# One adjacency load, one-operation masks, blockwise-turned exponentials and a re-planned order in a four-layer graph network

## The chip, the cores and the metric

The kernel runs on one core of one Trainium2 chip. The metric is the time of one execution on the device in microseconds (us). The core has five engines with a queue each: TensorE (PE, matmul), VectorE (DVE), ScalarE (ACT), GpSimd (POOL) and SyncE (SP), which here issues nearly all DMA transfers. Each engine works through its queue in order.

## The reference

128 graphs of 64 nodes with 256 features, `x` [128, 64, 256], and an integer adjacency `adj` [128, 64, 64] with entries 0 or 1. Four layers follow each other; each takes `h = relu(layernorm(x))` and adds its result to `x`:

```
layer 0  Wh = h W (4 heads of 64); e = leaky_relu(e_src[i] + e_dst[j], 0.2)
         e = where(adj > 0, e, -1e9); x += elu(softmax(e) Wh)
layer 1  the same with one head of 256 and -9e15
layer 2  relational convolution over relations 1 to 40; with entries of 0 and 1 only
         relation 1 is present: relu(adjT @ ((hW + b) * sigmoid(hWg + bg)))
layer 3  three rounds: aggr = AT (h weight_i); h = GRU(aggr, h)
out = x + h
```

All is float32. The kernel checks the adjacency's largest entry at the end and would redo everything on a general path (`general`, L1643) if it were above 1; with these inputs it is not entered.

## The kernel before

**Tiling.** Two graphs lie in one tile of 128 partitions, four such tiles make a group (`G = 4`, eight graphs), and 16 groups make the batch. Every group passes layers 0, 1 and 2 and then the three steps of the recurrence (layer 3). The steps of two neighbouring groups are interleaved: `(g, 0), (g-1, 2), (g, 1)` and so on, while the first three layers of later groups run in the gaps. The last group's steps come at the end.

**The order of the work is planned when the kernel is built.** The program's operations are recorded by `Plan.note` (the class `Plan`), each with a cost from `cost` (L583). `forward` (L328) places them engine by engine, choosing among ready operations the one with the earliest due time; `backward` (L427) derives new due times from the placement; `emit` (L503) repeats this `PASSES` times with a random generator started at `SEED` (L281), keeps the shortest plan, shifts the ranks of jobs by the listed `MOVES` (seeds for `move`, L474), places once more and issues the result. A transfer occupies SP for `ISSUE` = 665 ns in the plan and then one common wire for its bytes divided by a rate (L591). As the operations are issued from `emit`, the profile gives L549 for most of them; the products that use quarters of the array side by side are issued from `beside` (L841).

**Filler.** Where the plan foresees idle time of PE in its first 115 us, `emit` issues matmuls on a constant tile `warm` (L530, the matmul itself is L1638), whose results nobody reads: one for each 220 ns of the idle time less 100 ns.

**Loads.** `load_group` (L1298) loads a group's rows `xg` and its adjacency `at`, with the graphs of a tile pair arranged as `(t r a)`, in four transfers of 32 KB; three buffers. `load_edges` (L1312) loads the adjacency a second time as `ag`, in the order of `xg` (one transfer of 128 KB, four buffers), and a third time, transposed, as `eg`. `at` goes into the masks of layers 0 and 1, `ag` into `abd`, the recurrence's matrix (`before_recurrence`, L968).

**Masks.** `edge_bounds` (L1365) makes from `at` a matrix `m` that is `BIG` at an edge and 0 elsewhere (or `TINY` in a row without any edge). Layers 0 and 1 take the minimum of the exponentials and of `m` transposed (`mt`). It takes five VectorE operations: the row maximum `top`, its maximum `amax` for a final check of the adjacency's range, the test `top`, the product `m`, and the maximum of both.

**Exponentials.** `attention` (L1383) takes the scores `es` of the sources and targets of a group (`values`, L867, product with `w0e` or `w1e`). `exp(max(a, 0.2 a))` with `a = src + dst` is built from factors `fs`, `fd`, `gd`. For the first two groups the source factor is spread over partitions by a matmul. For the other 14 groups it is turned: ACT makes `fs` [128, n heads], PE transposes it (`tp<-ident,fs`), VectorE copies it as `fT` out of PSUM, one transfer stores `row` in DRAM, and two read it back, each for 64 partitions, as `t`. Then VectorE multiplies by `gd`, takes the maximum with `fd` and the minimum with `mt` (`t<-t,gd`, `t<-t,fd`, `t<-t,mt`), and PE multiplies with the values (`mm<-wh,t` and `mn<-wh,t`, `aggregate_graphs`, L909).

**Start.** Before the recurrence can start, group 0 passes its three layers in two halves (the second half's tiles end in `e`), and the weights of the recurrence are transposed and multiplied (`hhn`, `ihn`, `wrn`, `gn`; products `mm<-ihT,gT`). The recurrence's products go to PSUM banks `sy` and `sz`. The layer norm of the first two groups is turned by PE (`tp<-ident,hn`), that of later ones by VectorE and DMA (`way`, `hn`).

Of the kernel before, what the change touches and what calls it, by code (L numbers as in the profile page):

```python
# [10 lines left out]
F32 = mybir.dt.float32  # L11
I32 = mybir.dt.int32
# [15 lines left out]
NEG1 = -9000000000000000.0  # L28
ALPHA = 0.2
EPS = 1e-5  # L30
BIG, TINY = 3.0e38, 1.0e-24
BOUND = 6.25
NREL = 39
RC = 5
# [188 lines left out]
class Plan:  # L223
# [30 lines left out]
    def note(self, engine, call, cost, writes, reads, after=(), port=0.0, dma=False):  # L254
# [23 lines left out]
            b.ops.append(op)  # L278
        return op

    PASSES, SEED, SPREAD = 27, 39, 50.0  # L281
    MOVES = (
        10, 12, 18, 24, 27, 28, 58, 71, 83, 84, 89, 99, 118, 129, 136, 141, 144, 198, 214, 221, 266, 299, 322, 324,
        334, 341, 346, 390, 400, 412, 424, 434, 550, 559, 579, 611, 616, 682, 785, 808, 825, 869, 910, 1123, 1323,
        1710, 1729, 1754, 1784, 1908, 1924, 1933, 2133, 2158, 2174, 2755, 2883, 3921, 3988, 4026, 4270, 4596, 4876,
        4885, 5049, 5501, 5547, 5750, 5954, 6055, 6156, 6434, 6590, 7283, 7340, 7414, 7540, 7602, 7657, 7774, 7857,
        7930, 7942, 8201, 8457, 8683, 8685, 9083, 9436, 9811, 9967, 10320, 10820, 10999, 11484, 11701, 12627, 12696,
        12718, 12783, 12858, 12980, 13024, 13178, 13347, 13474, 14022, 14057, 14422, 14846, 16253, 16751, 16786,
        17194, 18227, 19571, 21611, 22526, 22951, 22990, 23107, 24055, 25299,
    )  # L290
    LEEWAY = {"PE": 100.0, "DVE": 100.0, "Activation": 100.0, "Pool": 100.0, "SP": 300.0, "-": 0.0}
    OVERLAP = {"DVE": 83.0, "Activation": 95.0, "Pool": 43.0}
# [210 lines left out]
    def emit(self):  # L503

        self.on = False
        self.link()
        best, self.random = None, Random(self.SEED)
        for _ in range(self.PASSES):
            ranks = [op.due for op in self.ops]
            end, order = self.forward()  # L510
            if best is None or end < best[0]:
                best = end, ranks, [op.start for op in self.ops]
            self.backward(end)
        end, ranks, starts = best
        jobs = list({id(op.job): op.job for op in self.ops}.values())
        for j in jobs:
            j.sum, j.count, j.shift = 0.0, 0, dict.fromkeys(self.RANKED, 0.0)
        for op, start in zip(self.ops, starts):
            op.job.sum, op.job.count = op.job.sum + start, op.job.count + 1
        for m in self.MOVES:  # L520
            self.move(m, end, jobs)
        for op, due in zip(self.ops, ranks):
            op.due = due + op.job.shift.get(op.engine, 0.0)
        end, order = self.forward()
        best = end, [(op, op.start, op.idle, op.places) for op in order]
        self.ends = best[0]
        for op, start, idle, places in best[1]:
            op.start = start
            if op.engine == "PE" and self.spare and start < 115.0 * 1e3:
                for _ in range(int((idle - 100.0) / 220.0)):  # L530
                    self.spare()
            for b, tag in places:
                b.pool.make(b, tag)
            op.call()
        self.ops = []
        return best[0]
# [46 lines left out]
def cost(engine, method, args, kwargs):  # L583

    n = elements(args[0])
    if engine == "tensor":
        m = elements(args[2] if method == "matmul" else args[0])
        return (m / 1.2 + 2.5) * (1 if method == "transpose" else 2)
    if engine == "sync" or method == "dma_start":
        to, of = args[:2]  # L590
        rate = {"way": 450.0, "fine": 220.0}.get(to.base.tag, 150.0) if isinstance(to, View) else 150.0  # L591
        if isinstance(of, View) and of.base.tag in ("way", "fine"):
            rate = 170.0 if of.base.tag == "way" else 125.0
        return n * to.shape[0] * 4 / rate
    if engine == "vector":
        if method == "bn_stats":
            return 400.0
        if method == "tensor_reduce":
            n = elements(args[1])
        plain = method == "tensor_scalar" and not any(isinstance(a, View) for a in args[2:4])  # L600
        return 150.0 + n * (0.53 if plain and n >= 512 else 1.04)
    if engine == "scalar":
        return 150.0 + 0.86 * n if method in ("copy", "mul") else 310.0 + 0.73 * n
    if ALU.pow in args:
        return 1000.0
    return 200.0 + 2.1 * n if method != "memset" else 100.0 + 0.85 * n
# [3 lines left out]
def kernel(  # L610
# [33 lines left out]
    xr = x.rearrange("b n d -> (b n) d").rearrange("(t q) d -> q t d", q=P)  # L644
    ar = adj.rearrange("b n m -> (b n) m").rearrange("(t q) m -> q t m", q=P)

    tr = adj.rearrange("(t r a) i j -> t a i r j", r=2, a=2)
    er = adj.rearrange("(t r a) j i -> t r j a i", r=2, a=2)
    outr = out.rearrange("b n d -> (b n) d").rearrange("(t q) d -> q t d", q=P)

# [7 lines left out]

    same = nc.kept(const, [P, P], F32, name="same")
    diag = nc.kept(const, [P, N], F32, name="diag")  # L660
    amax = nc.kept(const, [P, NG], F32, name="amax")
    flag = nc.kept(const, [1, 1], I32, name="flag")
    wc = nc.kept(const, [P, LAYERS, K, 3 * D], F32, name="wc")
    whh = nc.kept(const, [P, K, 3 * D], F32, name="whh")
# [554 lines left out]
    with ExitStack() as s1:  # L1219
# [47 lines left out]
        class Layer:  # L1267
# [2 lines left out]

            place = {"em": "hn", "dg": "hn", "tb": "hn", "land": "hn"}

            shared = {"hn": 3, "o": 2, "st": 4, "mv": 4, "var": 4, "rstd": 4, "nm": 4, "rec": 4, "fT": 1}

            def __init__(self, layer, pool, bufs):
                self.layer, self.pool, self.bufs = layer, pool, bufs
# [16 lines left out]
        for i, a in enumerate((a_src, a_dst)):  # L1293
            nc.scalar.dma_start(AB[:, i, :], over_partitions(a, D))
        nc.scalar.dma_start(w0e[:, :, :D], rows(W0))
        AT, XG, AG, EG = [], [], [], []

        def load_group(g):  # L1298
            nc.begin(("load", g))
            xg = work.tile([P, G, D], F32, name="xg", bufs=5)  # L1300
            n = 2 if g == 0 else G
            for p in range(0, G, n):
                nc.sync.dma_start(xg[:, p : p + n], xr[:, g * G + p : g * G + p + n, :])
            at = work.tile([P, G // 2, 2, N], I32, name="at", bufs=3)
            for a in range(2):
                for u in range(G // 2):
                    edges = tr[g * G // 2 + u, a]
                    nc.sync.dma_start(at[a * N : (a + 1) * N, u], edges)
            AT.append(at)
            XG.append(xg)  # L1310

        def load_edges(g):  # L1312
            ag = work.tile([P, G, N], I32, name="ag", bufs=4)
            nc.sync.dma_start(ag, ar[:, g * G : (g + 1) * G, :])
            AG.append(ag)
            eg = work.tile([P, G, N], I32, name="eg", bufs=2)
            for r in range(2):
                for u in range(G // 2):
                    nc.sync.dma_start(eg[r * N : (r + 1) * N, 2 * u : 2 * u + 2], er[g * G // 2 + u, r])
            EG.append(eg)  # L1320
# [44 lines left out]
        def edge_bounds(g):  # L1365


            at = AT[g]
            top = work.tile([P, G // 2, 2], F32, name="top")
            nc.vector.tensor_reduce(top, at, AX.X, ALU.max)  # L1370
            nc.vector.tensor_reduce(amax[:, g : g + 1], top, AX.XY, ALU.max)
            nc.vector.tensor_scalar(top, top, 0.0, TINY, op0=ALU.is_le, op1=ALU.mult)
            m = work.tile([P, G // 2, 2, N], F32, name="m", bufs=1)
            nc.vector.tensor_scalar(m, at, 0.0, BIG, op0=ALU.is_gt, op1=ALU.mult)
            nc.vector.tensor_tensor(m, m, top[:, :, :, None].to_broadcast([P, G // 2, 2, N]), ALU.max)
            pt = psum.tile([P, T], F32, name="tp")
            for u in range(G // 2):
                nc.tensor.transpose(pt[:, u * P : (u + 1) * P], m[:, u].rearrange("p g j -> p (g j)"), ident)
            mt = work.tile([P, G, N], F32, name="mt", bufs=3)
            nc.scalar.copy(mt.rearrange("p g i -> p (g i)"), pt[:, : G * N])  # L1380
            return mt

        def attention(g, p0, n, layer, heads, we, pool):  # L1383
# [31 lines left out]
                    )  # L1415
            else:

                fs = pool.tile([P, n, heads], F32, name="fs")
                nc.scalar.activation(fs, es[:, :, :heads], AF.Exp, scale=ALPHA - 1.0)
                pt = psum.tile([P, T], F32, name="tp")  # L1420
                nc.tensor.transpose(pt[:nh, :P], fs.rearrange("p g h -> p (g h)"), ident)
                fT = pool.tile([nh, P], F32, name="fT")
                nc.vector.tensor_copy(fT, pt[:nh, :P])
                row = dram.tile([2, nh * N], F32, name=f"row{layer}")
                nc.sync.dma_start(row.rearrange("a (c i) -> c a i", i=N), fT.rearrange("c (a i) -> c a i", i=N))
                for half in range(2):
                    nc.sync.dma_start(
                        t[half * N : (half + 1) * N].rearrange("p c i -> p (c i)"),
                        row[half : half + 1, :].to_broadcast([N, nh * N]),
                    )  # L1430
            flat = lambda d, c: d.rearrange("p g h -> p (g h)")[:, c, None].to_broadcast([P, len(range(nh)[c]), N])
            m = 2 if heads > 1 else n
# [95 lines left out]
        def before(g):  # L1528
            ABD[g] = work.tile([P, G, N], F32, name="abd")
            by_dma = dram if g >= AHEAD else None  # L1530
            START[g] = before_recurrence(W[3], psum, XG[g], AG[g], ABD[g], by_dma, g in PLAIN)

        def recur(g):
            return Recurrence(
# [321 lines left out]
```

## Time and profile before

| what | us |
|---|---|
| median of three timed runs | 1317.81 |
| lowest and highest of them | 1317.18, 1320.26 |
| profiled execution | 1316.05 |
| its span, first to last instruction | 1314.2 |
| granted TensorE clock in it | 0.998 |

The profile is of one execution. Its page gives, for every engine, the busy time and its share of the span; then the chain of work that ended last, followed back from the end, with each engine's share; then groups of instructions with their mean duration, and the idle time just before them with what ended it. The view of waits lists who waited for whom: total us, how often, the longest. The timeline gives start and length of merged instructions, with the idle time before the first in brackets. The view by stage gives, for a stretch of time, its length and then each engine's busy us (and instructions) in the order PE, PE's weight loads, DVE, ACT, POOL, then the granted clock, the share of DMA and its GB/s. PE runs a float32 product in two passes, so the profile counts most matmuls twice.

### The profile page before, as it was taken

To read this page: it belongs to the slowest core of one execution; us is meant where nothing else is said; L and a number is where in the kernel's file an instruction comes from. 1 tells how busy PE (TensorE), PEld (TensorE's weight loads), DVE (VectorE), ACT (ScalarE), POOL (GpSimd) and SP (SyncE) were. 2 spreads that over 40 slices of the span, in tenths; PEclk is the share of its full clock that TensorE was granted. 3 is DMA by queue.
4 is the path that set the end of the run, shared out by engine and by line. 5 is a ranking of instruction groups with operands and counts; after the bars stand their busy time and mean duration, and the time that the engine had idled before them with its cause. 6 is when DMAs were issued, how large, how long until landed. Compare 5 with 4: busy or idle time off the path is not lost.

```text
span 1314.2 us, 27889 instructions
## 1 busy us (share of the span) xinstructions
PE 1298.9 (99%) x9837; PEld 1030.0 (78%) x9837; DVE 1058.3 (81%) x2562; ACT 856.6 (65%) x2173; POOL 694.3 (53%) x845
## 2 busy tenths in 40 slices
PE   9999999999999999999999999999999999999997
PEld 8667887878787777878778787877878788778885
DVE  6878667978879798897968889796887979786666
ACT  5867765666776676667766666776666667645543
POOL 2745744646555545546535564654556447445453
PEclk9999999999999999999999999999999999999999
DMA  7232122335334343443434344334334423142222
GB/s 229 66 101 58 53 85 89 110 121 161 110 117 143 115 138 94 144 122 116 126 118 142 92 150 120 104 122 132 113 104 143 132 86 129 38 129 65 65 65 68
DMA packets 132782, 144.94 MB, mean 110 GB/s; under 512 B 43417, under 2 KB 117913, under 8 KB 132633
## 3 DMA queue, kind: packets, MB, share of 16 engines
q1 hardware_dynamic: 132072, 142.54, 35.8%
q8 instruction: 80, 1.31, 0.4%
q10 hardware_dynamic: 560, 0.52, 0.1%
q14 instruction: 70, 0.57, 0.1%
HBM read 81.01 MB, written 61.49 MB: 108 GB/s over the span
## 4 chain that ended last, share of the span: by engine, by line
PE 85%; DVE 5%; ACT 5%; POOL 2%; issue 1%; DMA 1%; SPq 0%; ACTq 0%; DVEq 0%; POOLq 0%
PE sy L549 34%; PE sz L549 25%; PE mm L549 15%; PE mm L841 3%; PE tp L841 3%; ACT hn L549 2%; DVE hT L549 2%; PE sz L1638 1%; PE tp L549 1%; DVE t L549 1%; ACT hT L549 1%; PE tq L841 1%; DVE r L549 1%; POOL rstd L549 1%; DVE st L549 1%
## 5 line engine op out<-in xcount | busy, mean ns | idle before, releaser
L549 POOL TENSOR_TENSOR r<-hT,hT 128x256 f32<-128x256 f32 x192 | 156.2, 820 | 274.9 <-ACT hT L549 273.6
L549 DVE SCALAR_TENSOR_TENSOR hT<-r,hT 128x256 f32<-128x256 f32 (+1 forms) x290 | 182.4, 633 | 26.8 <-ACT r L549 24.5
L549 PE MATMUL sy<-hS,wsum 128*128 128x256 f32 x576 | 172.4, 383 | 1.2 <-ACT r L549 0.7
L549 PE MATMUL sy<-aS,wsum 128*128 128x256 f32 x576 | 172.4, 382 | 0.0
L549 PE MATMUL sz<-hS,whh 128*128 128x256 f32 x576 | 171.4, 383 | 0.6 <-DVE z L549 0.6
L549 PE MATMUL sz<-aS,wc 128*128 128x256 f32 x576 | 167.0, 383 | 0.8 <-DVE hT L549 0.8
L549 DVE TENSOR_TENSOR hT<-hT,sz 128x256 f32<-128x256 f32 x288 | 118.2, 410 | 39.5 <-PE sz L549 32.9
L549 ACT ACTIVATE hT<-hT,bi 128x256 f32<-128x256 f32 x192 | 95.7, 505 | 61.9 <-DVE hT L549 60.8
L549 POOL TENSOR_TENSOR aS<-aT 128x256 f32<-128x256 f32 x96 | 82.5, 859 | 94.0 <-ACT aT L549 94.0
L549 PEld LDWEIGHTS sy<-hS,wsum 128*128 128x128 f32 x576 | 106.8, 190 | 30.4 <-issue 9.4
L549 PEld LDWEIGHTS sy<-aS,wsum 128*128 128x128 f32 x576 | 107.6, 190 | 21.1 <-issue 4.2
L549 PEld LDWEIGHTS sz<-hS,whh 128*128 128x128 f32 x576 | 106.4, 190 | 22.4 <-issue 5.2
L549 PEld LDWEIGHTS sz<-aS,wc 128*128 128x128 f32 x576 | 106.9, 190 | 17.8 <-DVE hT L549 1.2
L549 ACT ACTIVATE hn<-xg,nm,rstd 128x256 f32<-128x256 f32 x200 | 108.0, 592 | 19.6 <-POOL nm L549 18.3
L549 ACT ACTIVATE hT<-sy,bh 128x256 f32<-128x256 f32 x192 | 90.2, 470 | 45.6 <-PE sy L549 42.4
L549 POOL TENSOR_TENSOR rstd<-var,mhalf 128x4 f32<-128x4 f32 (+1 forms) x70 | 78.1, 1115 | 77.0 <-ACT var L549 76.8
L549 PE MATMUL mm<-wl,hT 128*128 128x512 f32 x248 | 118.6, 594 | 0.0
L549 ACT COPY z<-sy 128x256 f32<-128x256 f32 x192 | 70.4, 367 | 64.9 <-PE sy L549 63.7
L549 DVE TENSOR_TENSOR hT<-hT,sy 128x256 f32<-128x256 f32 x192 | 79.3, 413 | 36.3 <-PE sy L549 34.1
L549 DVE BATCH_NORM_STATS2 st<-xg 128x6 f32<-128x256 f32 x256 | 96.3, 408 | 8.2 <-POOL xg L549 4.8
L549 DVE TENSOR_TENSOR z<-sz,z 128x256 f32<-128x256 f32 x192 | 79.5, 415 | 28.7 <-PE sz L549 27.2
L549 POOL TENSOR_TENSOR hS<-hT 128x256 f32<-128x256 f32 x96 | 80.0, 834 | 38.1 <-DMA hT<-way 15.2
(207 smaller groups left out, 3212.6 us busy)
## 6 DMA issues: line engine op xcount, KB each, us to landing
way<-tb SPq DMA_DIRECT2D x59, 512.0 KB, 2.7
hnat<-way SPq DMA_DIRECT2D x184, 128.0 KB, 3.0
way<-hn SPq DMA_DIRECT2D x42, 512.0 KB, 3.0
hn<-way SPq DMA_DIRECT2D x168, 128.0 KB, 3.1
xg<-in_x_dram SPq DMA_DIRECT2D x15, 512.0 KB, 4.4
out_dram<-xg SPq DMA_DIRECT2D x15, 512.0 KB, 2.9
t<-row SPq DMA_DIRECT2D x28, 256.0 KB, 4.1
hT<-way SPq DMA_DIRECT2D x52, 128.0 KB, 2.8
```

What stands on the lines that cost most here:

```text
L549: return do(*[real(a) for a in args], **{k: real(v) for k, v in kwargs.items()})
L841: nc.nc.tensor.matmul(*[real(x) for x in product], start=True, stop=True)
L1638: nc.spare = lambda: psum.spare and nc.nc.tensor.matmul(pause, warm, warm, start=True, stop=True)
```

## The change

The adjacency is loaded once per group, as `at` in the order of `xg`, in one transfer with six buffers; `ag` is gone and the recurrence reads `at`. `edge_bounds` regroups `at` as a view, writes the row maxima straight into a wider `amax`, and makes `m` with one operation, adjacency times `BIG`, maximum with `top`; `BIG` is 1e29 instead of 3e38. In `attention`, `fs` becomes a tile of 32 columns that holds the exponentials of all of `es` (sources and targets; the targets' are not read), the rest set to zero by POOL; VectorE transposes its blocks of 32 into `fT`, four transfers store its four blocks of partitions in `row`, and the two reads of `t` take the sources' part of it. The planner gets other transfer rates, more passes, another seed and other moves, and its filler in the first 12 us counts 280 ns each.

```diff
-    PASSES, SEED, SPREAD = 27, 39, 50.0
-    MOVES = (10, 12, 18, 24, 27, 28, ...)
+    PASSES, SEED, SPREAD = 40, 37, 50.0
+    MOVES = (10, 28, 49, 52, 99, 112, ...)
...
-                for _ in range(int((idle - 100.0) / 220.0)):
+                for _ in range(int((idle - 100.0) / (280.0 if start < 12e3 else 220.0))):
...
-        rate = {"way": 450.0, "fine": 220.0}.get(to.base.tag, 150.0) if isinstance(to, View) else 150.0
+        tag = to.base.tag if isinstance(to, View) else None
+        rate = {"way": 450.0, "fine": 220.0, "t0": 190.0, "t1": 190.0}.get(tag, 150.0 if tag in (None, "at", "eg", "o", "row0", "row1") else 290.0)
...
-            at = work.tile([P, G // 2, 2, N], I32, name="at", bufs=3)
-            for a in range(2):
-                for u in range(G // 2):
-                    edges = tr[g * G // 2 + u, a]
-                    nc.sync.dma_start(at[a * N : (a + 1) * N, u], edges)
+            at = work.tile([P, G, N], I32, name="at", bufs=6)
+            nc.sync.dma_start(at, ar[:, g * G : (g + 1) * G, :])
...
-            ag = work.tile([P, G, N], I32, name="ag", bufs=4)
-            nc.sync.dma_start(ag, ar[:, g * G : (g + 1) * G, :])
-            AG.append(ag)
...
-            nc.vector.tensor_reduce(top, at, AX.X, ALU.max)
-            nc.vector.tensor_reduce(amax[:, g : g + 1], top, AX.XY, ALU.max)
-            nc.vector.tensor_scalar(top, top, 0.0, TINY, op0=ALU.is_le, op1=ALU.mult)
+            nc.vector.tensor_reduce(most, at, AX.X, ALU.max)
+            nc.vector.tensor_scalar(top, most, 0.0, TINY, op0=ALU.is_le, op1=ALU.mult)
             m = work.tile([P, G // 2, 2, N], F32, name="m", bufs=1)
-            nc.vector.tensor_scalar(m, at, 0.0, BIG, op0=ALU.is_gt, op1=ALU.mult)
-            nc.vector.tensor_tensor(m, m, top[:, :, :, None].to_broadcast([P, G // 2, 2, N]), ALU.max)
+            nc.vector.scalar_tensor_tensor(
+                m.rearrange("p u r j -> p (u r) j"), AT[g], BIG,
+                top.rearrange("p u r -> p (u r)")[:, :, None].to_broadcast([P, G, N]), op0=ALU.mult, op1=ALU.max,
+            )
...
-                fs = pool.tile([P, n, heads], F32, name="fs")
-                nc.scalar.activation(fs, es[:, :, :heads], AF.Exp, scale=ALPHA - 1.0)
-                pt = psum.tile([P, T], F32, name="tp")
-                nc.tensor.transpose(pt[:nh, :P], fs.rearrange("p g h -> p (g h)"), ident)
-                fT = pool.tile([nh, P], F32, name="fT")
-                nc.vector.tensor_copy(fT, pt[:nh, :P])
-                row = dram.tile([2, nh * N], F32, name=f"row{layer}")
-                nc.sync.dma_start(row.rearrange("a (c i) -> c a i", i=N), fT.rearrange("c (a i) -> c a i", i=N))
+                fs = pool.tile([P, S], F32, name="fs")
+                used = 2 * nh
+                if used < S:
+                    nc.gpsimd.memset(fs[:, used:], 0.0)
+                nc.scalar.activation(fs[:, :used], es.rearrange("p g h -> p (g h)"), AF.Exp, scale=ALPHA - 1.0)
+                fT = pool.tile([P, S], F32, name="fT")
+                nc.vector.transpose(fT, fs)
+                row = dram.tile([2, S // (2 * heads), 2, heads * N], F32, name=f"row{layer}")
+                for q in range(P // S):
+                    nc.sync.dma_start(
+                        row[q // 2].rearrange("x s (h i) -> (x s h) i", i=N)[:, q % 2 * S : (q % 2 + 1) * S],
+                        fT[q * S : (q + 1) * S],
+                    )
                 for half in range(2):
                     nc.sync.dma_start(
-                        t[half * N : (half + 1) * N].rearrange("p c i -> p (c i)"),
-                        row[half : half + 1, :].to_broadcast([N, nh * N]),
+                        t[half * N : (half + 1) * N].rearrange("p (g h) i -> p g (h i)", h=heads),
+                        row[half : half + 1, :n, 0].to_broadcast([N, n, heads * N]),
                     )
...
-            START[g] = before_recurrence(W[3], psum, XG[g], AG[g], ABD[g], by_dma, g in PLAIN)
+            START[g] = before_recurrence(W[3], psum, XG[g], AT[g], ABD[g], by_dma, g in PLAIN)
```

## The prediction

> **What bounds the kernel now.** I read the page from the top: busy times, then the chain, then the waits of TensorE (PE) alone, then the start by time.
>
> ```profile
> PE 1298.9 (99%) x9837; PEld 1030.0 (78%) x9837; DVE 1058.3 (81%) x2562; ACT 856.6 (65%) x2173; POOL 694.3 (53%) x845
> ...
> PE 85%; DVE 5%; ACT 5%; POOL 2%; issue 1%; DMA 1%; SPq 0%; ACTq 0%; DVEq 0%; POOLq 0%
> ```
>
> PE is busy nearly all the time and is 85% of the chain that ends last. Matmul spans overlap, so I do not trust 99% alone; the waits decide.
>
> ```profile
> PE tp L549 <- DVE hT L549: 1.9, 3, 1.2
> PE sy L549 <- DVE hT L549: 1.4, 1, 1.4
> PE sz L1638 <- DVE mhalf L549: 1.1, 1, 1.1
> PE sz L549 <- DVE hT L549: 0.8, 1, 0.8
> ```
>
> All of PE's waits sum to about 9 us in 1314, so for most of the run each of its instructions starts as soon as the one ahead lets it. The time is therefore PE's work plus whatever stands in its queue that is no work. That filler is the `warm` matmul of L1638, and it lies at the start:
>
> ```profile
> 1.06 11.23 PE L1638 MATMUL sz<-warm 128*128 128x128 f32 x80 [1.06 <-DVE mhalf L549]
> 12.13 0.60 PE L549 MATMUL tp<-ident,hn 128*128 128x128 f32 x4
> 12.57 2.62 PE L1638 MATMUL sz<-warm 128*128 128x128 f32 x22
> 15.02 0.61 PE L549 MATMUL mm<-w0e,hT 128*128 128x264 f32 x2
> ...
> 6.88 1.09 ACT L549 ACTIVATE hn<-xg,nm,rstd 128x256 f32<-128x256 f32 x2 [1.11 <-POOL nm L549]
> ...
> 12.77 0.66 ACT L549 ACTIVATE hT<-tp 128x256 f32<-128x256 f32 x2 [4.51 <-PE tp L549]
> ```
>
> The first rows `hn` are there at 6.88 + 1.09 = 7.97, but PE turns them only at 12.13, when its 80 filler passes are through; ScalarE (ACT) then has waited 4.51 us for PE. The filler was emitted for an idle time that the planner foresaw, and it outlasts it. By stage:
>
> ```profile
> 0.00:15.00 15.00, 13.94 (x106) 13.94 (x107) 7.82 (x30) 4.68 (x11) 2.66 (x14) 1.00 0.78 211
> 15.00:105.70 90.70, 88.80 (x628) 59.83 (x626) 73.42 (x232) 70.96 (x229) 47.63 (x79) 1.00 0.40 110
> 105.70:1298.00 1192.30, 1189.43 (x9077) 951.72 (x9077) 967.83 (x2282) 777.06 (x1927) 640.10 (x748) 1.00 0.36 110
> ```
>
> The columns after the length are busy us of PE, weight loads, VectorE (DVE), ACT and GpSimd (POOL). From 105.9, where the first recurrence matmul (`sy<-hT,whh`) starts, PE lacks 3 of 1192 us. Time is to be won in the first 106 us, or by taking PE instructions out.
>
> **What the Trainium skill says.** "Perfetto Trace Analysis", Identifying the Most-Contended Engine: matmul busy share is no measure of headroom; hence I price PE by start-to-start times. "TensorE: Matmul & The Clock Gate", What's actually happening: the array runs at half clock until about 3.4 us of activity. The trace agrees: the filler passes start 0.213 us apart until 5.28, then 0.111. "VectorE: DVE Perf Modes", The three transpose paths: VectorE turns 32x32 blocks, not the whole 128 partitions; so the turned tile has to leave as four pieces. "DMA: Bandwidth & Descriptors", Why small descriptors are slow (HBM only): a 256-byte descriptor bears 27% of bus overhead, and a fixed fee. No row of the trace shows `t` fetched in such pieces.
>
> **The change part by part.** Prices of PE from the trace: 216 ns start to start for each of the two passes of a 256-column product, 109 ns for a 128-column transposition.
>
> *Transpositions of `fs`.* 28 of them (14 groups, two layers) leave PE, on the path everywhere after 100 us: 28 x 0.109 = 3.05 us. For them VectorE copies 28 x (0.271 and 0.265) = 7.5 us out of PSUM; it now turns 28 tiles of 128x32. Its transpositions took 693 ns for 512 elements and 1240 for 1024, a line that gives 0.15 + 32 x 0.00107 = 0.18 us: 5.1 us. VectorE has 19% free, so this is worth nothing by itself.
>
> ```profile
> L549 PE MATMUL tp<-ident,fs 128*16 128x128 f32 x14 | 3.8, 273 | 0.0
> ...
> L549 DVE STREAM_TRANSPOSE tb<-hT 128x512 f32<-128x512 f32 x92 | 63.0, 693 | 1.9 <-DMA way<-tb 1.5
> ```
>
> *Masks.* Per group 0.409 + 0.145 + 0.225 + 0.366 + 0.498 = 1.64 us of VectorE become 0.41 + 0.23 and one two-operand operation of 256 elements (`hT<-r,hT`: 0.54): 1.18. Sixteen groups: 7.4 us of VectorE. On no path after 106 us; before it, a few tenths, taken as 0.
>
> *Adjacency once.* 64 `at` loads of 32 KB and 16 `ag` loads leave, 16 of 128 KB come. About 0.65 us of SyncE's (SP) queue each: 80 to 16 issues. The queue also gets 112 `row` transfers for 28. `row<-fT` held it 0.30 us each, so +25 us against some -40 us: SP is no worse. At the start it matters: `hhn` was issued at 13.3 behind eight small loads, and now stands tenth.
>
> *Memset and longer exponentials.* 14 memsets of 0.10 us on POOL wait for VectorE's reading of the same buffer one group (some 80 us) earlier: no wait. Behind them stand POOL's subtractions `r<-hT,hT`, which see 0.1 us; ACT's exponential waits for the memset, done long before. 0.
>
> *The plan.* The list of moves, its seed and the transfer rates re-order all queues, which the diff does not price; the built order does. Up to the first `sy` the program before holds 84 fillers and 76.5 us of other PE work at the prices above; the changed one 55 fillers and 73.8 us (some layer-three work moves behind that point). First stretch: 28 fillers instead of 40. By the start times of the trace the 57th pass starts at 9.45, and the first `hn` is ready at 7.97. Then two transposition pairs, three fillers (six passes of 0.11) and two of `gn`: 9.45 + 0.44 + 0.67 + 0.44 + 0.22 = 11.2. ACT's second `hn` (ready about 10.3) and the first copies `hT` (0.66) end at 11.0; the second half of the columns of `w0e` now stands on VectorE behind group 1's statistics, about 11.1 by its rows. So `mm<-w0e` starts near 11.3 instead of 15.02, with 0.66 us more work behind it.
>
> Rest of the start: before, 105.91 - 15.02 = 90.9 us held 76.0 us of work, 33 fillers x 0.22 = 7.3, and 7.6 us of idle and switching. After: 73.8 - 1.1 = 72.7 of work, 24 fillers = 5.3, and the same 7.6: 85.6. First `sy` at 96.9, 9.0 us earlier. From there on PE's work is 1166.2 us against 1166.6: the 3.05 us won is nearly all given back by the moved work. Sum: -9.4 us. The 7.6 us is my choice; it could be 4.5 (each gap filled as closely) to 11 (the planner's faster transfers do not come true).
>
> *Exponentials' turn-round.* The chain from the copy `es` to the product `wh,t` loses the matmul and a PSUM copy and gains three issues. Layer one, near 286 us:
>
> ```profile
> 286.44 0.23 ACT L549 ACTIVATE fs<-es 128x4 f32<-128x4 f32 x1
> 287.66 0.27 DVE L549 COPY fT<-tp 4x128 f32<-4x128 f32 x1
> 287.96 0.26 SPq L549 DMA_DIRECT2D row<-fT  x1
> 289.14 1.12 SPq L549 DMA_DIRECT2D t<-row  x2
> 292.36 0.43 DVE L549 TENSOR_TENSOR t<-t,gd 128x256 f32<-128x256 f32 x1 [0.32 <-DMA t<-row]
> ```
>
> `fs` to `row` was 1.5 us and becomes about 0.9; the fourth `row` is issued 0.9 later; `t` lands later by 0 to 1.5 (four times as many pieces), taken 0.4: +0.7 us. In PE work, the smallest distance from layer one's `w1e` product to its `wh,t` in steady groups was 9.0 us and becomes 10.2. It fits, with 0.5 us to spare. I take 0; range 0 to 5.
>
> Against the profiled execution: 1316.05 us = span 1314.2 + 1.9 around it, and 1316.05 - 9.4 = 1306.6. The median of the timed runs is 1.8 us above that execution: 1308.4. I forecast 1308.0.
>
> **Rivals.** *Start bound by its chain.* Group 0 has to pass three layers before the first `sy`; if the 91 us from `w0e` to `sy` are latency, only the first shift counts: -3.7 - 0.4, 1313.7 from the median. For it: ACT and DVE are 78 and 81% busy there. Against: PE lacks under 2 us in that stage, and fewer fillers were needed. Loads later than the plan's new 290 GB/s (the trace has 355 in full stretches, 211 over the first 15 us) end here too.
>
> *Slower: the four-piece turn.* If `t` lands 2.5 us later in its 256-byte pieces (1 KB in layer zero), layer one's chain outgrows 10.2 us by some 2.5 and the 11 us of the middle group by 1.7. PE, in order, stands for that in about 12 groups: +20 us, 1317.8 - 9.4 + 20 = 1328. It decides from a stand of 0.8 us a group. Against: the skill's 27% on a landing of 2.6 us is 0.7. Layer zero had 2 to 4 us between landing and use.
>
> *More.* If idle falls to 4.5 and the last 17 us, half idle, shorten too: 1304.
>
> **How the numbers follow.** Forecast 0.64, chain-bound start 0.20, slower 0.11, more 0.05. About 0.3% (4 us) can be told from no change: faster is below 1313.9, slower above 1321.8. The chain-bound case straddles the first bound, 0.12 of it below. Faster 0.81, same 0.08, slower 0.11. The range 1303.5 to 1316 leaves out the slower case and slivers.
>
> **What would show it.** Right: `mm<-w0e` at 11 to 11.6; first `sy` at 95 to 99; 110 filler passes; no PE wait on `DVE t` over 1 us. Wrong: first `sy` after 101 (chain), or PE `mm` of the small products waiting for `DVE t` behind `DMA t<-row` in every group (slower). PE waits of several us after the first `sy` of any other kind would disprove the sum.

## The result, and the profile after

The changed kernel takes 1314.16 us (median of 8 runs, 1312.61 to 1316.42), the kernel before 1317.57 (8 runs, 1316.68 to 1320.26): ratio 0.9976, interval 0.9966 to 0.9985. That is 3.4 us less, where the sum had 9.4. The profiled execution took 1314.07 us, span 1312.2 + 1.9: 2.0 us less than that of before, which at 1316.05 was quicker than all eight of these runs.

The page, busy times and the chain:

```profile
PE 1291.7 (98%) x9751; PEld 1023.4 (78%) x9751; DVE 1058.9 (81%) x2530; ACT 854.6 (65%) x2173; POOL 690.8 (53%) x859
...
PE 86%; DVE 3%; ACT 2%; POOL 2%; issue 1%; DMA 1%; SPq 0%; DVEq 0%; ACTq 0%; POOLq 0%
```

PE lost 7 us of busy time, but the span only 2.0. The start, PE first, then VectorE, by start time, duration and instruction:

```profile
1.06 8.09 PE L1640 MATMUL sz<-warm 128*128 128x128 f32 x56 [1.06 <-DVE warm L1638]
8.99 0.82 PE L550 MATMUL tp<-ident,hn 128*128 128x128 f32 x4
...
12.47 1.13 PE L550 MATMUL mm<-w0e,hT 128*128 128x264 f32 x4 [1.09 <-ACT nm L550]
```

```profile
9.90 0.75 DVE L550 BATCH_NORM_STATS2 st<-xg 128x6 f32<-128x256 f32 x2 [0.78 <-DMA xg<-in_x_dram]
...
11.70 0.67 DVE L550 TENSOR_REDUCE w0e<-wa 128x8 f32<-128x512 f32 x1
```

56 filler passes instead of 80 stand ahead of the first transposition. `mm<-w0e` starts at 12.47 instead of 15.02; what it waits for is VectorE's second half of the columns of `w0e`, ended at 12.37 (the 1.09 put down to ACT is not it). The first recurrence product `sy<-hT,whh` starts at 98.23, before at 105.91. So the start won 7.7 us in these two executions, and the rest gave most of it back. By stage, busy us of PE, weight loads, VectorE, ACT and GpSimd after the length:

```profile
15.00:105.70 90.70, 89.58 (x673) 60.93 (x672) 76.94 (x216) 74.81 (x238) 59.19 (x88) 1.00 0.35 98
105.70:1298.00 1192.30, 1183.35 (x8972) 946.58 (x8970) 965.37 (x2260) 768.82 (x1910) 625.14 (x751) 1.00 0.36 108
```

From 105.7 on PE lacks 8.95 us of 1192, where it lacked 2.87. PE's waits from 106 to 1298 us, kernel before and changed kernel:

```profile
PE sy L549 <- DVE hT L549: 1.4, 1, 1.4
PE sy L549 <- ACT r L549: 0.7, 2, 0.5
PE sy L549 <- ACT z L549: 0.2, 1, 0.2
PE mm L841 <- DVE t L549: 0.2, 1, 0.2
```

```profile
PE sz L550 <- DVE hT L550: 3.6, 4, 1.7
PE sy L550 <- ACT z L550: 1.7, 2, 0.9
PE sy L550 <- DVE hT L550: 1.3, 2, 1.0
PE mm L842 <- ACT r L550: 0.6, 1, 0.6
```

The table shows the four largest of each. Most are waits of the recurrence (`sy`, `sz`), for several producers, each at another place. None is for `t`.

**A count used below.** For each PE instruction I take the time to the next one's start, and for each form (shape and what follows; a chain of small products as one) its usual value, the 30th percentile. The sum of the usual values is *work*; what goes beyond is *stands*. From the first `sy` to the last recurrence product, in us. The count is of one execution, the profiled one; its time and the median of the timed runs stand beside it:

```
                          first sy    work   stands  profiled   median
before                      105.91   1188.36   10.1    1316.1    1317.6
changed                      98.23   1188.04   16.4    1314.1    1314.2
e1_early                     98.47   1188.04   14.1    1312.1    1313.4
e2_whole                     99.31   1188.03   13.9    1312.7    1312.7
e3_fill220                   99.63   1188.03   18.3    1317.1    1317.0
e4_pool                      97.72   1188.09    6.9    1304.2    1304.9
e5_before_pool              105.27   1188.41    6.5    1312.1    1312.1
e6_before_fill280           104.40   1188.36   10.2    1315.6    1316.3
e7_more28                    98.86   1190.43   17.9    1318.7    1318.2
e8_long                      98.52   1188.09   20.3    1318.7    1316.5
e9_refit                    101.39   1188.98    9.2    1310.8    1311.4
e10_other                    98.29   1190.24   20.7    1321.6    1321.6
e11_before_refit            108.49   1187.18   15.5    1323.2    1322.6
e12_longer                  100.72   1188.90   12.8    1313.9    1315.8
e13_late                     98.39   1188.04   18.1    1315.9    1315.9
e14_before_late             106.55   1188.36    8.6    1315.2    1314.8
```

First `sy` -7.7, work -0.3, stands +6.3: -1.7 us, and the spans differ by 2.0. But the profiled execution of before was 1.5 us quicker than its median, and that of the changed kernel was not. For the medians (-3.4) the same sum leaves -7.7 - 0.3 + 4.6: between typical executions the stands grew by some 4.6 us, an estimate. In the same way `e8_long`'s stands are nearer 18 at its median and `e12_longer`'s nearer 15. The level of the stands depends on what is taken as usual; the differences between rows are what counts. Expectations written between 106 and 1280 us call the same stands 8.2 (before) and 14.2 (changed).

### The profile page after: what moved, and what is told of

It is laid out like the page before. It is cut to its first block, busy times and chain, and to the rows that moved or that the text cites. A ratio compares the mean times of both kernels' runs of the same rounds, so it can differ in the third digit from the quotient of the medians.

```text
span 1312.2 us, 27657 instructions
## 1 busy us (share of the span) xinstructions
PE 1291.7 (98%) x9751; PEld 1023.4 (78%) x9751; DVE 1058.9 (81%) x2530; ACT 854.6 (65%) x2173; POOL 690.8 (53%) x859
## 4 chain that ended last, share of the span: by engine, by line
PE 86%; DVE 3%; ACT 2%; POOL 2%; issue 1%; DMA 1%; SPq 0%; DVEq 0%; ACTq 0%; POOLq 0%
PE sy L550 37%; PE sz L550 27%; PE mm L550 14%; PE mm L842 3%; PE tp L842 3%; DVE hT L550 1%; ACT hn L550 1%; POOL xg L550 1%; PE tq L842 1%; DMA t<-row 1%; PE tp L550 0%; DVE hn L550 0%; PE mn L842 0%; ACT hT L550 0%; DVE t L550 0%
## 5 line engine op out<-in xcount | busy, mean ns | idle before, releaser
L550 POOL TENSOR_TENSOR r<-hT,hT 128x256 f32<-128x256 f32 x192 | 153.2, 804 | 241.0 <-ACT hT L550 237.3
L550 DVE SCALAR_TENSOR_TENSOR hT<-r,hT 128x256 f32<-128x256 f32 (+1 forms) x290 | 186.0, 648 | 27.9 <-ACT r L550 26.0
L550 POOL TENSOR_TENSOR aS<-aT 128x256 f32<-128x256 f32 x96 | 79.4, 828 | 105.2 <-ACT aT L550 105.1
L550 PEld LDWEIGHTS sy<-hS,wsum 128*128 128x128 f32 x576 | 106.3, 190 | 31.4 <-issue 10.1
L550 POOL TENSOR_TENSOR xg<-xg,hn 128x1024 f32<-128x1024 f32 (+1 forms) x32 | 76.3, 2384 | 44.7 <-DVE hn L550 44.7
```

The costliest lines, as they stand in the source:

```text
L550: return do(*[real(a) for a in args], **{k: real(v) for k, v in kwargs.items()})
```

## The experiments

The kernel before was timed again beside every experiment; its median moved between 1317.2 and 1318.4. Where a microsecond counts, I compare the ratios.

My first theory was the exponentials' turn-round: VectorE now waits for `t` where it hardly did. From 106 to 1298 us, before and after:

```profile
DVE t L549 <- DMA t<-row: 1.4, 2, 1.1
```

```profile
DVE t L550 <- DMA t<-row: 8.3, 7, 3.1
```

The rivals were the fillers at the start, VectorE's columns of `w0e`, and GpSimd's long additions, beside which VectorE's operations take longer.

**e1_early.** `t` is read from `x`, so that it need not wait for `row`; the exponentials of the sources are left out of the result:

```
- nc.sync.dma_start(t[half ...], row[half : half + 1, :n, 0].to_broadcast([N, n, heads * N]))
+ other = bass.AP(tensor=x.tensor, offset=x.offset, ap=[[0, N], [2 * heads * N, n], [1, heads * N]])
+ nc.note("SP", lambda to=to, other=other: nc.nc.sync.dma_start(real(to), other), ...)
```

> The changed kernel in its own order, but the two reads of t take constants from x in DRAM (pieces of 1 KB and 256 bytes, as many as before) and so need not wait for the four row transfers; the exponentials of the sources in layers 0 and 1 are left out of the result from group 2 on. If the four-piece turn is what holds PE up after the first sy (theory turn), t lands over 1 us earlier, VectorE's 8.6 us of waiting for t<-row go to under 2, PE's lack between 106 and 1298 us falls from 8.9 to 4 or less, and the time by 4 to 6 us, to about 1309. If the lack comes from an order that is packed so tightly that any of several late engines stops PE (theory packed), only the stalls behind t<-row go: PE lacks 7 to 8 us and the time falls by 0.5 to 2 us.

1313.40 us, ratio 0.9966 (0.9953 to 0.9978). **e2_whole** reads `t` in one contiguous piece per partition, with other contents:

```
+ flat_of = row[half : half + 1].rearrange("a x s f -> a (x s f)")[:, : nh * N].to_broadcast([N, nh * N])
```

> The changed kernel in its own order, but t is read from row as one contiguous piece of 4 KB or 1 KB per partition in place of four of 1 KB or 256 bytes; it still waits for the rows, and takes sources and targets mixed, so that the exponentials are wrong. This undoes the small pieces alone. Theory turn, if pieces are the cause: layer one's landing falls from 2.9 to about 2.6 us, VectorE's waits for t<-row by half, the time by 2 to 3 us. Theory packed: within 1 us of the changed kernel.

1312.65 us, 0.9966 (0.9956 to 0.9976). Both are some 0.1% (1.3 us) below the changed kernel's 0.9976, with intervals that overlap its own; their stands are 2.3 and 2.5 us fewer. VectorE waits almost as long as before even for a transfer that depends on nothing (e1_early, 106 to 1298 us):

```profile
DVE t L550 <- DMA t<-in_x_dram: 7.0, 6, 2.9
```

In layer one, `t` lands this long after its issue in the kernel before, the changed kernel and e2_whole (last column, median us):

```profile
t<-row SPq DMA_DIRECT2D x28, 64.0 KB, 2.6
t<-row SPq DMA_DIRECT2D x28, 64.0 KB, 2.9
t<-row SPq DMA_DIRECT2D x28, 64.0 KB, 2.8
```

The smaller pieces are thus 0.1 us of the 0.3. The turn-round costs some 1 to 2 us, which these runs hardly tell from nothing, and the pieces nothing that can be told. The theory falls. Both kernels kept the 112 issues of `row` in SP's queue; these were not tried apart.

**e3_fill220** takes the changed kernel's filler rule back; **e6_before_fill280** gives the new rule to the kernel before, whose order stays:

```
e3:  (idle - 100.0) / (280.0 if start < 12e3 else 220.0)   ->   (idle - 100.0) / 220.0
e6:  (idle - 100.0) / 220.0   ->   (idle - 100.0) / (280.0 if start < 12e3 else 220.0)
```

> The changed kernel with fillers of the first 12 us again counted 220 ns each; the plan knows nothing of fillers, so only their number changes (35 for 28 at the start). If the shorter filler is what brings the start forward, as the prediction had it (theory filler), mm<-w0e comes 1.5 us later and so does the end: +1.5 us. If VectorE's columns of w0e set that point (theory columns: they were ready at 12.4, and the first hn was turned at 9.2), the seven extra fillers of 0.22 us lie in front of it unseen: within 0.5 us of the changed kernel.

> The kernel before, in its own order, with the changed kernel's rule for the fillers of the first 12 us and nothing else: 31 fillers instead of 40 ahead of the first transposition. If the fillers hold PE at the start, the nine cost 18 x 0.111 = 2.0 us there and the time falls by that, to about 1315.7, with no new stand later. If the start is a chain of latencies, the 2 us are lost again before the first recurrence product: 1317.7.

e3: 1317.03 us, 0.9990 (0.9983 to 0.9997): slower than the changed kernel by 1.8 us by the ratios. e6: 1316.32, 0.9988 (0.9982 to 0.9995): 1.6 us won, with no more stands. The starts of eight profiled executions, in us from the first instruction; the filler passes are those ahead of the first transposition, and up to the time in the second column they start some 0.22 us apart, later 0.11:

```
                     passes  0.22 until  first tp  mm<-w0e  first sy
before                 80       5.28       12.13    15.02    105.91
e5_before_pool         80       3.99       11.47    14.37    105.27
e14_before_late        80       6.75       12.78    15.68    106.55
e6_before_fill280      62       6.50       10.63    13.53    104.40
changed                56       4.41        8.99    12.47     98.23
e2_whole               56       6.76       10.11    12.63     99.31
e13_late               56       6.77       10.15    12.54     98.39
e3_fill220             72       4.21       10.73    12.92     99.63
```

In the old order the three times move together: the filler passes set the start, and e6 won 1.5 us where 2.0 were expected because its slow passes lasted 1.2 us longer than in the profiled execution of before. In the new order they do not. The first transposition comes at 8.99 to 10.15 us, `mm<-w0e` always near 12.5: VectorE's columns of `w0e` hold it. e3's passes bring the transposition 1.7 us later and `mm<-w0e` only 0.4, against theory filler. But its time rose by more than the 0.5 us that theory columns allowed. Its first `sy` is 1.4 us later; without the extra fillers that lies at 98.2 to 99.3, so how much of e3's loss the fillers make stays open. So the new rule is worth 1.5 us in the old order. Of the start's 7.7 us, the 58 filler passes that the changed kernel has fewer (168 before, 110 now) account for some 6.5 at 0.112 us each, an estimate; 18 of them are the new rule's (e3, e6), the other 40 went because the new plan leaves less idle time.

**e4_pool.** GpSimd's long additions into `xg` add one row of four, or two:

```
- engine.tensor_tensor(src, src, em, ALU.add)
+ nc.nc.gpsimd.tensor_tensor(*[real(v[:, 0:1]) for v in (src, src, em)], ALU.add)
...
- nc.gpsimd.tensor_tensor(to, to, spread(self.hnat), ALU.add)
+ nc.nc.gpsimd.tensor_tensor(*[real(v[:, 0:2]) for v in (to, to, by)], ALU.add)
```

> The changed kernel in its own order, but POOL's long additions to x (1024 elements, 2.4 to 2.5 us, once per layer and group and once at a group's end) add a quarter of their elements only; three quarters of those sums are left out. At least three of PE's stalls after 106 us (at 254, 607 and 642 us) have such an addition in front of VectorE's late instruction. Theory packed: with the commonest late engine made early, PE's lack falls from 8.9 to about 5 us and the time by 3 to 4. Theory turn: no change beyond 1 us, as t<-row is untouched.

1304.92 us, 0.9904 (0.9887 to 0.9921): 9.2 us below the changed kernel, more than twice what was expected. One stand shows how. Changed kernel, GpSimd, VectorE and PE near 254 us:

```profile
251.56 2.80 POOL L550 TENSOR_TENSOR xg<-xg,hn 128x1024 f32<-128x1024 f32 x1
```

```profile
254.39 1.25 DVE L550 STREAM_TRANSPOSE hn<-hn 128x1024 f32<-128x1024 f32 x1 [2.25 <-POOL xg L550]
255.56 0.38 DVE L550 TENSOR_TENSOR hT<-hT,sz 128x256 f32<-128x256 f32 x1
```

```profile
253.74 0.61 PE L550 MATMUL mm<-w0e,hT 128*128 128x264 f32 x2
256.09 0.67 PE L550 MATMUL sz<-hS,whh 128*128 128x256 f32 x2 [1.74 <-DVE hT L550]
```

The addition runs 2.80 us; VectorE's transposition waits 2.25 us for it; behind that, in VectorE's order, stands `hT<-hT,sz`, on which PE's next `hS` hangs: PE stands 1.74 us. With the cut (e4_pool) VectorE waits 0.63 us and PE goes on:

```profile
252.23 1.25 DVE L550 STREAM_TRANSPOSE hn<-hn 128x1024 f32<-128x1024 f32 x1 [0.63 <-POOL xg L863]
```

```profile
253.20 0.61 PE L550 MATMUL mm<-w0e,hT 128*128 128x264 f32 x2
253.93 0.67 PE L550 MATMUL sz<-hS,whh 128*128 128x256 f32 x2
```

**e5_before_pool** makes the same cut in the kernel before.

> The kernel before, in its own order, with the same cut as in e4_pool: GpSimd's additions of four or two 256-wide rows into xg (43 of 2.4 us) add only one row, or two, so the output leaves a part of the residual sums out. If these additions are what any order pays for, the kernel before gains what the changed one gained, about 10 us: 1308. If it is the new order that lets them stand in PE's way, the kernel before gains little: PE's stands between 106 and 1280 us sum to 8.2 us in it against 14.2 in the changed kernel, and I expect 2 to 4 us: about 1315.

1312.13 us, 0.9955 (0.9941 to 0.9968): about 6 us less, between the two expectations. Both held in part: any order pays for these additions, and the new one pays some 3 us more by the medians. By the stands of the profiled executions it is 5.9 (10.1 to 6.5 in the old order, 16.4 to 6.9 in the new one), because that of before was a quick one. Cut, the two orders stand nearly alike, and the change is worth 1312.1 - 1304.9 = 7.2 us (7.7 by the spans, 6.7 by the ratios), where it is worth 3.4 with the additions whole.

**e8_long** asks whether the additions cost because GpSimd and `xg` are held so long, or because VectorE's operations take longer beside them. Ahead of each cut addition GpSimd does five operations of four elements:

```
+ nc.nc.gpsimd.tensor_tensor(some[:, :4], real(of), some[:, 4:], ALU.mult)
+ nc.nc.gpsimd.tensor_tensor(some[:, :4], some[:, 4:], some[:, 4:], ALU.pow)
+ for _ in range(3): nc.nc.gpsimd.tensor_tensor(some[:, :4], some[:, 4:], some[:, 4:], ALU.mult)
```

> e4_pool again, but each shortened addition of GpSimd is preceded by five operations of four elements (a product that reads the first values of the tile to be added, one power, three products), so that GpSimd is held for about 2.4 us from the same moment as in the changed kernel, and xg is complete as late as there[...]. The output leaves the same residual sums out as e4_pool. If PE stands because xg and what is queued on GpSimd come 1.6 us later, this runs like the changed kernel: about 1314. If it is the long two-operand VectorE operations that GpSimd slows beside its additions, this runs like e4_pool: about 1305.

1316.45 us, 0.9989 (0.9982 to 0.9995). VectorE is as fast as in e4_pool. Changed kernel, e4_pool and e8_long, with mean ns after the busy us:

```profile
L550 DVE SCALAR_TENSOR_TENSOR hT<-r,hT 128x256 f32<-128x256 f32 x196 | 105.4, 544 | 27.2 <-ACT r L550 26.0
```

```profile
L550 DVE SCALAR_TENSOR_TENSOR hT<-r,hT 128x256 f32<-128x256 f32 x196 | 90.8, 469 | 28.9 <-ACT r L550 27.6
```

```profile
L551 DVE SCALAR_TENSOR_TENSOR hT<-r,hT 128x256 f32<-128x256 f32 x196 | 90.9, 470 | 27.3 <-ACT r L551 26.1
```

Yet it is 2.3 us slower than the changed kernel (1.7 by the ratios). GpSimd is busy 2.74 us for each of the 43 additions (summed over the six groups), and 3.00 from the start of the first operation to the end of the last, against 2.49 in the changed kernel and 0.85 in e4_pool. A line through the last two puts 2.74 at 1315.6 and 3.00 at 1317.0, an estimate; the measured time lies between. So the hold of GpSimd and of `xg` is enough for the loss; VectorE's slower operations are not needed for it.

**e7_more28** puts 28 transpositions back on PE by issuing each of the `m` of groups 2 to 15 twice.

```
+ if nc.on and g > 1:
+     once = nc.ops[-1].call
+     nc.ops[-1].call = lambda once=once: (once(), once())
```

> The changed kernel with 28 more transpositions of 128 columns on PE: those of the masks m of groups 2 to 15 are issued twice, in the same order of everything else. They stand for the 28 of fs that the change took away. If PE's work counts in full, the time rises by 28 x 0.109 = 3.05 us, to 1317.2. If PE's stands after the start take them up, it rises by less than 1.5 us.

1318.24 us, 1.0002 (0.9993 to 1.0010): +4.1 by the medians, +3.4 by the ratios. First `sy` +0.6 (six of the 28 stand ahead of it), work +2.4: 3.0 together, as 28 x 0.109 says. PE's work counts in full. The count has 1.5 us of stands on top; one execution does not tell whether the shift makes them.

**New orders of the same work.** Was the changed order made from durations that are too short? In both traces ScalarE's normalizations start 491 ns apart where the planner's costs make it 402, GpSimd's powers 1.09 us where they make it 0.96, and many loads land 0.3 us later. e9_refit starts from the finished plan, corrects these costs and tries further moves; e12_longer tries more of them; e11_before_refit does it to the kernel before; e10_other keeps the costs and takes other moves.

```
+ if abs(c - 496.88) < 1.0 and tag in ("hn", "hnat", "hnat3"):
+     c = 587.0
...
+ c += 130.0 if c == 1000.0 else 30.0 if abs(c - 2350.4) < 1 else 0.0
...
+ Plan.LAND = 250.0
...
+ for m in self.AGAIN:
+     self.move(m, end, jobs)
```

> The changed kernel with the same instructions, ordered once more. The planner starts from the changed kernel's finished plan, its costs are set to what the traces show (normalizations on ScalarE 587 ns for 497, the power on GpSimd 1130 for 1000, its 1024-element additions 30 more, every landing 0.25 us later, a few smaller ones), and 4,600 further random moves are tried against these, of which 72 shorten its plan and are kept. If the stands after the start come of an order made from durations that are too short, they fall from 14.2 to about 6 us and the time to 1306 (1303 to 1309). If they belong to the work, or if the start is spoilt by the new order, 1312 to 1316.

> The changed kernel with its own costs, unchanged, but another list of moves: 5,300 other random draws, from the same start, of which 72 are kept. The planner's own end is 5 us later than that of the changed kernel's list. If too short durations leave every such order with stands in places of its own, this has 10 to 16 us of them after the start as well: 1313 to 1319. If the changed kernel's list is a bad draw, this one is faster than it: under 1310.

> The kernel before, ordered once more in just the way of e9_refit, with 4,600 draws of which 71 are kept. Its stands after the start are 8.2 us and should fall to 4 or 5: 1313. The difference to e9_refit is then what the change is worth when both orders allow for the same durations: by my forecast 9 us; if the change has no such gain in it, 3 us as measured.

> e9_refit with 10,600 draws, of which 105 are kept; the planner's end is 2.2 us earlier. If the refitted plan is to be trusted, it is 1 to 3 us faster than e9_refit. If its last gains only fit the planner's own errors, it is the same within 1 us.

e9: 1311.44 us, 0.9962 (0.9948 to 0.9976), stands 9.2, the fastest here with full work. It is 5.4 us above the 1306 expected, 3.2 of them a later start (30 filler passes more). e10: 1321.55, 1.0038 (1.0024 to 1.0052), stands 20.7: worse than I expected, but its plan already ended 5 us later and it has 24 filler passes more, so only a part is a surprise. e12: 1315.75, 0.9993 (0.9985 to 1.0001): the longer search, better by its own plan, is 4 us worse than e9. e11: 1322.61, 1.0038 (1.0024 to 1.0052), stands up to 15.5: against the theory. A second draw of each, with the start left alone, was to decide (the diff is e9's, with costs changed only after 112 us, and other draws):

> The changed kernel with its start left as it is: durations as refitted for e9_refit, but only for what its plan starts after 112 us, and 4,300 other draws of moves, of which 86 are kept, that shift nothing of the first 125 us. So the first recurrence product stays near 98.2 us. If durations that are too short make the stands, those after the start fall again from 16.4 to about 9, and the time to 1307: start gain and gapless rest together, as forecast. If e9_refit was a lucky order, the stands end anywhere from 9 to 20: 1307 to 1318, with no reason for the lower end.

> The kernel before treated as e13_late: start left as it is, the same refitted durations after it, 4,300 draws of the same seeds, of which 79 are kept. In e11_before_refit its stands rose from 10.1 to 15.5 us although the durations were the refitted ones. If the refit is what counts and that was a bad draw, they are at most 10 now and the time 1317 or less; if the order decides by chance, 10 to 16: 1317 to 1323.

e13: 1315.89 us, 0.9989 (0.9981 to 0.9998), stands 18.1. e14: 1314.81, 0.9977 (0.9970 to 0.9984), stands 8.6. With refitted durations: 9.2, 12.8 and 18.1 in the changed kernel, 15.5 and 8.6 in the one before. The refit does not decide it; the theory falls too. What is shown is the spread: the same work, fillers apart, stands 9 to 21 us in another order, where executions of one order differ by up to 4 in time. Which property of an order makes it so was not found, and the cut of GpSimd's additions was not tried in these orders.

## Why the prediction was wrong, point by point

**The step that failed** is the one that said "From there on PE's work is 1166.2 us against 1166.6" and took that for time. The work was right (-0.3 for -0.4); that PE follows it without stands was not argued for the new order, only read from the old one's 9 us of waits. The new list of moves made another order, whose stands are 16.4 us instead of 10.1 in the profiled executions: -7.7 - 0.3 + 6.3 = -1.7. Between the medians they grew by some 4.6 us: of the 6.0 us missing from the forecast 9.4, 1.3 are the start and 4.6 these stands. The prediction named this itself as what would disprove the sum ("PE waits of several us after the first `sy` of any other kind"), but gave it no case and no chance. By e4 and e5 most of the extra stands are GpSimd's long additions: without them the orders differ by 0.4 us in the profiled executions. Why they fall worse in the new order is open.

**First stretch and fillers.** 28 fillers, as said; the first transposition at 8.99 (9.45 said) because its slow passes ended at 4.41 us, those of before at 5.28. The prediction took the slow passes to last about 3.4 us and found the trace agreeing; that trace has 4.2, from 1.06 to 5.28, and the 16 profiled executions have 2.9 to 5.9. It had PE, ScalarE's copies and the columns of `w0e` ready almost together (11.2, 11.0 and 11.1); the columns came last, at 12.37. `mm<-w0e` came 1.2 us later than the 11.3 said; 0.78 of it is the wait of group 1's statistics, ahead of these columns on VectorE, for their load. "Rest of the start" was 98.23 - 12.47 = 85.8 us for 85.6 said. So -7.7 for -9.0, and 110 filler passes as said. The chain-bound start (rival, 1313.7) did not occur, since the stretch behind `mm<-w0e` shortened by 5 us; that the time fell near it is chance.

**Transpositions of `fs`.** Right: 28 of them are 3.0 us on PE (e7). VectorE's blocks take 197 ns, said 180.

**Exponentials' turn-round.** The product `wh,t` never waited for VectorE's `t` over 1 us; VectorE itself waited 8.3 us for `t`, and some 1 to 2 us of that, hardly clear of noise, reached the end (e1, e2), where I took 0 in a range of 0 to 5. The four-piece rival at 1328 is refuted. In layer one `t` landed 0.3 us later than before, said +0.4; the pieces are 0.1 of it (e2), where the prediction's 27% gave an estimate of 0.7.

**Memset.** "No wait" was wrong: seven of the 14 waited for VectorE's `fT`, 12.8 us in sum, up to 4.0. No stand of PE was traced to it.

**Masks, adjacency.** The mask operation took 522 ns where 540 was used. VectorE's busy time did not fall (1058.3 to 1058.9 us): what the masks saved (some 7 us), other operations lost; `v` alone took 4 us more. No part of the result was traced to it, as said. SP issued `hhn` eleventh (tenth said), at 9.90 us, before at 13.26: no worse, as said.

## What to carry to other kernels

Where a change carries a new order with it, sum work and stands apart: the work can be counted from the built order, but the stands of a PE that is 99% busy belong to the order and do not carry over. Here orders of the same work spread over 12 us of stands, more than the change was worth. Look then for the longest operations of the engines that PE does not wait for by name: cutting one 2.5-us kind on a half-idle engine brought both orders to nearly the same stands. And compare the profiled execution with the median before a difference of stands is read as the kernel's own.

## What the runs showed of the hardware that I had not expected

- VectorE's two-operand operation of 256 elements takes 416 ns alone (median 418), and up to 2.52 us beside a long addition on GpSimd (at 1000.5 us of the changed kernel); 544 on average. PE's stands do not need it: they stay when it is reduced (e8).
- VectorE turns a 128x32 tile in 32x32 blocks in 197 ns.
- Fetching `t` in 256-byte pieces to 64 partitions from device memory took 2.9 us to land, in one piece each in the same order 2.8 (e2); in the old order it had been 2.6.
- PE's first matmuls run at half pace for a time that differs from execution to execution: in the 16 profiled ones the filler passes, which start at 1.06 us in each, go from 0.22 to 0.11 us apart at 3.99 (e5) to 6.98 us (e9). This alone moved the kernel before's first `sy` by 1.3 us.
